# Delta-rule layer: SiLU of the values by Tanh, issued with the convolution instead of behind the exponentials

## Chip, cores and metric

The kernel runs on one core of a Trainium2 chip. The metric is the device time of one execution in microseconds (us). The engines are TensorE (PE, with its weight loads as PEld), VectorE (DVE), ScalarE (ACT), GpSimd (POOL) and the DMA queues (SyncE issues most of them, SPq).

## What is computed

One decoder layer in fp32: a gated delta-rule layer, a cross-attention over 77 context rows, and a mixture of eight experts, each followed by a layer norm. Only the first part matters here. For x of 4 sequences (B), 1024 tokens and 256 channels:

```python
def causal_conv_silu(x, w):
    B, T, C = x.shape
    K = w.shape[1]
    xp = jnp.pad(x, ((0, 0), (K - 1, 0), (0, 0)))
    y = sum((xp[:, i:i + T, :] * w[:, i] for i in range(K)))
    return jax.nn.silu(y)
...
q = causal_conv_silu(normed @ Wq, conv_q)
k = causal_conv_silu(normed @ Wk, conv_k)
v = causal_conv_silu(normed @ Wv, conv_v)
beta = jax.nn.sigmoid(normed @ Wb)
g = -jnp.exp(A_log) * jax.nn.softplus(normed @ Wa + dt_bias)
```

q and k are normalised, and then, token by token, with a state S per sequence and head (4 heads, keys of 64, values of 128):

```python
S = S * jnp.exp(g_t)[..., None, None]
v_eff = (v_t - jnp.einsum('bhk,bhkv->bhv', k_t, S)) * b_t[..., None]
S = S + k_t[..., None] * v_eff[..., None, :]
o_t = jnp.einsum('bhk,bhkv->bhv', q_t, S)
```

The output o is normalised, multiplied by the SiLU of a gate, and projected.

## The kernel before

The delta rule is worked out in eight slabs of 128 tokens, all four sequences at once. Within a slab the recurrence becomes matrix work: a triangular matrix of decays and key products is inverted, and its inverse is multiplied with keys, values and the state.

Each slab goes through generator functions, whose pieces `interleave` takes in turn (L244), so that the program's order mixes several of them. For slab i there are two phases (L840 to L851):

- the first phase: `prepares(i + 1)` (decay factors, an Exp on ScalarE at L495, and the products bp on VectorE, L518), `inverts(i)`, and a chain of `decays(i + 2)`, `values(i)` and `cumulated(i + 2)`. `decays` and `cumulated` hold further small Exps (L358, L369, L400).
- the second phase: `scans(i)` (the recurrence with the state), `blocks(i + 1)` (a long chain of small VectorE operations), `project(i + 2)` (queries and keys) and `normed(i + 3)`. Its ScalarE functions that are neither copies, scalings nor squares are Silus: of keys and queries (L435) and of the gate (L765).

`values` makes four tiles v[0] to v[3], one for each head, of 128 channels by 4 x 128 tokens. `convolve` (L275) makes a tile in two halves: matmuls into a PSUM bank (L281), the first of four taps on ScalarE (L291, an Identity with a per-channel scale), the other three on VectorE (L293, `scalar_tensor_tensor` of 128x256, in place). The weights of the taps are columns of the tile `cols`, read by channel. The Silu of the values is not part of `values`: it is issued by `silus` (L471) after the whole first phase, at L847.

Every Exp of L400 and L495 is kept in the list `exps`, and `silus` puts its four Silus behind them on ScalarE:

```python
with ExitStack() as behind:
    for e in exps:
        behind.enter_context(tc.issue_after(e.ins))
    exps.clear()
    for v in made["v"]:
        nc.scalar.activation(v, v, AF.Silu)
```

The order of instructions on each engine is otherwise settled by the framework's scheduler, from the order of the program and from when it expects operands and buffers[...].

What takes up the values is `scan` (L631). It first transposes queries and keys into a bank (L640, ptok) and the values into another (L643, pv; one transpose for each of v[0] to v[3]). Then VectorE makes qk from ptok and the factors qw (L646, qw itself copied from the cumulated exponentials at L409 and L410); ScalarE makes kd (L654, from ptok) and vt (L658, from pv), four each; TensorE turns qk (L664, pqd) and multiplies it with the inverse (L673, pwt); ScalarE copies both into padded tiles (L685); and then the products with the state follow (L691 on).

Squares of keys and queries, and the square and gate of the output, use a common buffer tag `sqr` with three buffers.

Of the kernel before, what the change touches and what calls it, by code (L numbers as in the profile page):

```python
# [10 lines left out]
F32 = mybir.dt.float32  # L11
I32 = mybir.dt.int32
AF = mybir.ActivationFunctionType
ALU = mybir.AluOpType
# [3 lines left out]
P = 128  # L18
B, T, D = 4, 1024, 256
NS = T // P  # L20
KC = D // P
H, HK, HV = 4, 64, 128
DV = H * HV
NCH = (2 * D + DV) // P
NQK = 2 * D // P
KCONV = 4
# [30 lines left out]
C_CONV = 2 * KC  # L57
# [53 lines left out]
def kernel(ctx: ExitStack, tc: tile.TileContext, a: dict, out: bass.AP):  # L111
    nc = tc.nc
    mm = nc.tensor.matmul

    def bc(ap, shape):
        return ap.to_broadcast(shape)
# [5 lines left out]
    def bank(name, tag="bank", bufs=None):  # L122
        kw = {} if bufs is None else {"bufs": bufs}
        return ps_pool[0].tile([P, 512], F32, tag=tag, name=name, **kw)
# [9 lines left out]
    wk = scan_scope.enter_context(tc.tile_pool(name="dwk", bufs=2))  # L134
# [25 lines left out]
    cols = const.tile([P, NCOLS], F32, name="cols")  # L160
# [83 lines left out]
    def interleave(*gens):  # L244

        gens = list(gens)
        while gens:
            for g in list(gens):
                if next(g, gens) is gens:
                    gens.remove(g)  # L250
# [9 lines left out]
    nc.vector.tensor_scalar(nega, nega, 1e30, -1.0, ALU.min, ALU.mult)  # L260


    state = []
    for b in range(B):
        s = wp.tile([P, 2, HV], F32, tag=f"state{b}", name=f"state{b}")
# [3 lines left out]
    for j in range(4):  # L269
        z = wp.tile([P, H, P], F32, tag=f"pad{j}", name=f"pad{j}")  # L270
        nc.vector.memset(z, 0.0)
        padded.append(z)
    before, exps = [], []

    def convolve(dst, c, nT):  # L275

        w0 = C_CONV + c * KCONV
        for j in range(2):
            pp = bank("pp")
            for kc in range(KC):  # L280
                mm(  # L281
                    pp[:, 0 : 2 * (HALO + P)],
                    lhsT=wqkv[:, kc, c * P : (c + 1) * P],
                    rhs=nT[:, kc, 2 * j : 2 * j + 2, :].rearrange("p b t -> p (b t)"),
                    start=kc == 0,
                    stop=kc == KC - 1,
                )
            yield
            pre = pp[:, 0 : 2 * (HALO + P)].rearrange("p (b t) -> p b t", b=2)
            ch = dst[:, 2 * j : 2 * j + 2, :]  # L290
            nc.scalar.activation(ch, pre[:, :, 0:P], AF.Identity, scale=cols[:, w0 : w0 + 1])  # L291
            for n in range(1, KCONV):
                nc.vector.scalar_tensor_tensor(  # L293
                    ch, pre[:, :, n : n + P], cols[:, w0 + n : w0 + n + 1], ch, ALU.mult, ALU.add
                )
# [89 lines left out]
    def cumulated(made):  # L385

        g = made["g"]
        pd = bank("pd")
        for n, m in enumerate((le, gt, ones)):
            mm(  # L390
                pd[:, n * B * H : (n + 1) * B * H],
                lhsT=m,
                rhs=g.rearrange("p b h -> p (b h)"),
                start=True,
                stop=True,
            )
        yield
        ex = slab.tile([P, 3, B, H], F32, tag="ex", name="ex")
        exps.append(
            nc.scalar.activation(ex.rearrange("p n b h -> p (n b h)"), pd[:, 0 : 3 * B * H], AF.Exp)  # L400
        )
        el = slab.tile([P, B, 2], F32, tag="el", name="el")
        whole = ex[:, 2].rearrange("p b (r q) -> p b r q", q=2)
        for par in range(2):
            h0 = par * HK
            nc.vector.tensor_copy(el[h0 : h0 + HK], whole[h0 : h0 + HK, :, :, par])

        qw = slab.tile([P, B, 2, H], F32, tag="qw", name="qw")
        nc.vector.tensor_copy(qw[:, :, 0, :], ex[:, 0])  # L409
        nc.vector.tensor_scalar_mul(qw[:, :, 1, :], ex[:, 0], -1.0)  # L410

        made.update(ex=ex, el=el, qw=qw)
# [52 lines left out]
        made.update(kq=kq, nb=nb, cd=cd, ik=ik, eq=eq)  # L465

    def values(made):
        made["v"] = v = [slab.tile([P, B, P], F32, tag=f"v{c}", name="v", bufs=1) for c in range(H)]
        for c in range(H):
            yield from convolve(v[c], NQK + c, made["nT"])  # L470
    def silus(made):  # L471

        with ExitStack() as behind:
            for e in exps:
                behind.enter_context(tc.issue_after(e.ins))
            exps.clear()
            for v in made["v"]:
                nc.scalar.activation(v, v, AF.Silu)

    def work(name, shape, **kw):  # L480
        return wk.tile(shape, F32, tag=name, name=name, **kw)

    def prepare(i, b, made):

        g, kq = made["g"], made["kq"]
        ee = work("ee", [P, H, 2, P])
        nc.gpsimd.tensor_tensor(
            ee[:, :, 1, :], bc(le.unsqueeze(1), [P, H, P]), bc(g[:, b, :].unsqueeze(2), [P, H, P]), ALU.mult
        )
        yield  # L490

        pe = bank("pe")
        mm(pe, lhsT=gt, rhs=ee[:, :, 1, :], start=True, stop=True)
        exps.append(
            nc.scalar.activation(ee[:, :, 0, :], pe.rearrange("p (h t) -> p h t", h=H), AF.Exp)  # L495
        )
        nc.gpsimd.tensor_tensor(
            ee[:, :, 1, :], ee[:, :, 0, :], bc(nge.unsqueeze(1), [P, H, P]), ALU.mult
        )
        yield  # L500

        bp = made["bp"]
        pks = [bank("pk") for par in range(2)]
        for r in range(2):
            for par, pk in enumerate(pks):
                h0 = slice(par * HK, (par + 1) * HK)
                mm(
                    pk[:, r * 2 * P : (r + 1) * 2 * P],
                    lhsT=kq[r][h0, 0, b, :],
                    rhs=kq[r][h0, :, b, :],  # L510
                    start=True,
                    stop=True,
                )
        yield
        for par, pk in enumerate(pks):
            for r in range(2):
                h = 2 * r + par
                nc.vector.scalar_tensor_tensor(  # L518
                    bp[:, :, b * H + h],
                    pk[:, r * 2 * P : (r + 1) * 2 * P].rearrange("p (n t) -> p n t", n=2),  # L520
                    made["nb"][:, b, h : h + 1],
                    ee[:, h],
                    ALU.mult,
                    ALU.mult,
                )
# [268 lines left out]
    made = [{} for _ in range(NS)]  # L794
# [6 lines left out]
    def prepares(i):  # L801
        made[i]["bp"] = slab.tile([P, 2, B * H, P], F32, tag="bp", name="bp", bufs=2)
        made[i]["tt"] = tts[i % 2]
        gens = [prepare(i, b, made[i]) for b in range(B)]
        return [chain(*gens[n::2]) for n in range(2)]

    def inverts(i):
        return [invert(b, made[i]) for b in range(0, B, 2)]

    def scans(i):  # L810
        return [
            chain(scan(i, b, made[i]), scan(i, b + 1, made[i])) for b in range(0, B, 2)
        ]
# [4 lines left out]
    def some(f, i, *args):  # L818
        return [f(*args, made[i])] if i < NS else []
# [15 lines left out]
    interleave(*some(decays, 0, 0), *some(normed, 1, 1))  # L835
    keys0 = project(0, made[0])
    interleave(chain(islice(keys0, 5), *some(cumulated, 0), keys0), *some(decays, 1, 1))
    interleave(*prepares(0), *some(cumulated, 1), *some(normed, 2, 2))
    interleave(blocks(0, made[0]), *some(project, 1, 1))
    for i in range(NS):  # L840
        ahead = prepares(i + 1) if i + 1 < NS else []
        interleave(
            *ahead,
            *inverts(i),
            chain(*some(decays, i + 2, i + 2), values(made[i]), *some(cumulated, i + 2)),
        )
        silus(made[i])  # L847
        if i + 1 < NS:
            interleave(
                *scans(i), *some(blocks, i + 1, i + 1), *some(project, i + 2, i + 2), *some(normed, i + 3, i + 3)  # L850
            )  # L851
# [820 lines left out]
```

## Time and profile before

| | |
|---|---|
| median of 3 runs | 1769.08 us (1767.61 to 1770.75) |
| the profiled execution | 1769.31 us, of which the span 1767.5 us |
| delta-rule stage | from the start to about 760 us |
| VectorE, taps of the values (L293) | 192, mean 478 ns, 81.7 us |
| ScalarE, Silu of the values (L478) | 32, median 629 ns |
| ScalarE, table loads in front of L478 / L495 / L435 | 7 / 8 / 4, each 1283 ns |
| last Exps and Silu table loads by slab | loads at 138.3, 231.5, 322.4, 412.8, 504.5, 592.6, 671.3 us |

The span is the time from the first to the last instruction in the trace; the execution's time has a little more around it. A row of the profile names the line of the code, the engine, the operation, and the tiles that it writes and reads. The releaser behind an idle time is what ended it. Several instructions of one line that run in a row are shown as one row with their number, so that 7.13 us for x18 is the time of all eighteen.

### The profile page before, as it was taken

The page shows a single profiled execution, that of the slowest core. Times are in us where ns is not written, and L with a number is a line of the kernel's source. Part 1 is how long each engine was busy: PE and PEld are TensorE (multiplying, and loading weights), DVE is VectorE, ACT ScalarE, POOL GpSimd, SP SyncE. Part 2 cuts the span into 40 slices and gives each one's busy share as a digit, 9 for nine tenths or more (in the row PEclk, how much of TensorE's full clock was granted, in tenths as well). Part 3 has the DMA queues.
Part 4 walks back from the last instruction along what each step waited for, and adds up shares of the span by engine and source line. Part 5 has one row for each costly group of instructions (what it writes and reads, how often), then busy time and mean ns, then how long its engine had stood idle before and what let it go on. Part 6 is the DMA issues. An engine that isn't in the chain of part 4 may idle for free. (4 is left out here: it accounts for less than half of the span.)

```text
span 1767.5 us, 28455 instructions
## 1 busy us (share of the span) xinstructions
PE 1593.5 (90%) x9524; PEld 1154.2 (65%) x9524; DVE 1176.1 (67%) x3557; ACT 938.1 (53%) x2216; POOL 565.4 (32%) x486
## 2 busy tenths in 40 slices
PE   6659999999999999896889999999989999999991
PEld 4247777676767667773667778778856666666660
DVE  4657686878787875735366888888865655554554
ACT  4425555555555554551288888788843333333333
POOL 2311212121212121015045666566733322222222
PEclk9868999999989998998999999999999999999995
DMA  4011101010101010203130011111353332222226
GB/s 142 19 19 22 40 19 43 19 43 19 43 19 31 19 31 19 56 7 125 44 147 13 27 44 43 40 43 37 126 189 70 64 47 47 46 46 46 47 32 199
DMA packets 119023, 94.20 MB, mean 53 GB/s; under 512 B 56939, under 2 KB 108639, under 8 KB 118367
## 3 DMA queue, kind: packets, MB, share of 16 engines
q1 hardware_dynamic: 102383, 71.39, 14.3%
q0 software_dynamic: 13296, 17.83, 6.0%
q10 hardware_dynamic: 3200, 3.15, 0.6%
q8 instruction: 78, 1.28, 0.3%
q14 instruction: 66, 0.54, 0.1%
HBM read 55.46 MB, written 36.90 MB: 52 GB/s over the span
## 5 line engine op out<-in xcount | busy, mean ns | idle before, releaser
L1547 POOL DMA_INDIRECT xd<-my,mrow x71 | 110.5, 1557 | 295.0 <-ACT my L1546 266.1
L1116 ACT ACTIVATE sc<-sc,ntop,rq 128x77 f32<-128x77 f32 x512 | 182.4, 447 | 5.2 <-DVE ntop L1111 4.6
L1147 PE MATMUL pxo<-ball,aT 128*128 128x256 f32 (+1 forms) x640 | 151.9, 385 | 1.5 <-DVE xs L1158 1.5
L281 PE MATMUL pp<-nT,wqkv 128*128 128x262 f32 x512 | 151.5, 434 | 0.2 <-PE pu L613 0.2
L1077 POOL TENSOR_TENSOR rq<-rq,nhalf 128x8 f32<-128x8 f32 x64 | 106.7, 1668 | 130.3 <-DVE rq L1076 129.2
L1498 PE MATMUL pgt<-wall,mxT 128*128 x284 | 135.4, 599 | 0.0
L1498 PE MATMUL pup<-wall,mxT 128*128 x284 | 134.4, 596 | 0.0
L1525 PE MATMUL pdn<-wdn,mhT 128*128 x568 | 134.2, 379 | 0.0
L752 POOL TENSOR_TENSOR so<-so,nhalf 128x4 f32<-128x4 f32 x32 | 32.5, 1017 | 309.5 <-DVE so L751 309.5
L1147 PEld LDWEIGHTS pxo<-ball,aT 128*128 128x128 f32 (+1 forms) x640 | 118.1, 193 | 15.8 <-DVE xs L1158 2.1
L1060 PE MATMUL pq<-wdn,xT 128*128 128x512 f32 x256 | 120.6, 594 | 1.5 <-ACT qsq L1070 1.0
L281 PEld LDWEIGHTS pp<-nT,wqkv 128*128 128x128 f32 x512 | 99.9, 211 | 23.4 <-issue 5.1
L293 DVE SCALAR_TENSOR_TENSOR kq<-pp,cols,kq 128x256 f32<-128x256 f32 x192 | 88.6, 479 | 36.3 <-ACT kq L291 33.9
L1525 PEld LDWEIGHTS pdn<-wdn,mhT 128*128 128x128 f32 x568 | 102.5, 190 | 11.0
L1506 DVE TENSOR_TENSOR sge<-pgt,ball 128x512 f32<-128x512 f32 x71 | 49.1, 692 | 86.4 <-PE pgt L1498 85.6
L1507 ACT ACTIVATE sge<-sge 128x512 f32<-128x512 f32 x71 | 44.7, 630 | 112.5 <-DVE sge L1506 112.4
L1498 PEld LDWEIGHTS pup<-wall,mxT 128*128 128x128 f32 x284 | 54.5, 192 | 69.0 <-issue 69.0
L1508 DVE TENSOR_TENSOR pup<-pup,ball 128x512 f32<-128x512 f32 x71 | 49.7, 700 | 69.8 <-PE pup L1498 69.3
L1125 POOL TENSOR_TENSOR sc<-sc,den 128x616 f32<-128x616 f32 x64 | 78.1, 1221 | 55.0 <-DVE den L1124 50.3
L1546 ACT ACTIVATE my<-my,mw 128x256 f32<-128x256 f32 x71 | 36.1, 508 | 106.3 <-DVE my L1545 106.3
L293 DVE SCALAR_TENSOR_TENSOR v<-pp,cols,v 128x256 f32<-128x256 f32 x192 | 81.7, 478 | 14.0 <-ACT v L291 13.3
L1096 PE MATMUL psc<-wdn,qT 128*128 128x154 f32 x512 | 78.7, 296 | 7.2 <-ACT qT L1088 7.2
(314 smaller groups left out, 3705.5 us busy)
## 6 DMA issues: line engine op xcount, KB each, us to landing
mx<-xg SPq DMA_DIRECT2D x71, 130.0 KB, 2.1
xs<-xd SPq DMA_DIRECT2D x12, 512.0 KB, 10.6
xi<-in_x SPq DMA_DIRECT2D x8, 512.0 KB, 4.5
am<-ab SPq DMA_DIRECT2D x16, 256.0 KB, 3.8
xd<-kd SPq DMA_DIRECT2D x32, 128.0 KB, 1.7
wall<-in_L_ffn_gate_w SPq DMA_DIRECT2D x8, 512.0 KB, 9.6
wall<-in_L_ffn_up_w SPq DMA_DIRECT2D x8, 512.0 KB, 10.2
xd<-xs SPq DMA_DIRECT2D x8, 512.0 KB, 4.1
```

Source lines behind the costliest of these rows:

```text
L281: mm(pp[:, 0 : 2 * (HALO + P)], lhsT=wqkv[:, kc, c * P : (c + 1) * P], rhs=nT[:, kc, 2 * j : 2 * j + 2, :].rearrange("p b t -> p (b t)"), ...
L293: nc.vector.scalar_tensor_tensor(ch, pre[:, :, n : n + P], cols[:, w0 + n : w0 + n + 1], ch, ALU.mult, ALU.add)
L1060: mm(pq, lhsT=t["xT"][:, kc, :], rhs=xwq[:, kc, c0 : c0 + HH * XD], start=kc == 0, stop=kc == KC - 1,)
L1077: nc.gpsimd.tensor_tensor(rq, rq, nhalf[:, :HH], ALU.pow)
L1096: mm(ps[:, c * 2 * SC : (c + 1) * 2 * SC], lhsT=qT[:, 2 * g + c, :], rhs=kbd[:, b, half * XC // 2 + 2 * g + c, :], start=True, stop=True,)
L1116: nc.scalar.activation(sc[:, h], sc[:, h], AF.Exp, scale=t["rq"][:, h : h + 1], bias=t["ntop"][:, h : h + 1])
L1125: nc.gpsimd.tensor_tensor(sc, sc, bc(den.unsqueeze(2), [P, HH, SC]), ALU.mult)
L1147: mm(px[:, 0:D], lhsT=aT[:w, c, :], rhs=vo[:w, b, half * NV + c, :], start=half == 0 and c == 0, stop=half == 1 and c == NV - 1,)
L1498: mm(ps, lhsT=t["xT"][:, c, :], rhs=wall[:, bass.ds(e * EW + off + c * FF, FF)], start=c == 0, stop=c == KC - 1,)
L1508: nc.vector.tensor_tensor(pu, pu, ball[:, bass.ds(e * FF + B_U, FF)], ALU.add)
L1525: mm(px[:, 0:D], lhsT=t["hT"][:, f, :], rhs=wdn[:, bass.ds(e * EV + f * D, D)], start=f == 0, stop=f == FC - 1,)
L1547: nc.gpsimd.indirect_dma_start(out=xd, out_offset=bass.IndirectOffsetOnAxis(ap=row, axis=0), in_=y, in_offset=None, compute_op=ALU.add,)
```

## The change

The taps of the values are halved once at the start, so that `convolve` yields y, half of the convolution. The SiLU of 2y is y + y tanh(y). Right after each tile's convolution, inside `values`, a Tanh on ScalarE writes a new tile th (tag `sqr`), and a `scalar_tensor_tensor` on VectorE writes (th + 1) * v into v. The list of the exponentials and `silus` go.

```diff
--- before.py
+++ after.py
@@ -260,6 +260,10 @@
     nc.vector.tensor_scalar(nega, nega, 1e30, -1.0, ALU.min, ALU.mult)
 
 
+    vw = cols[:, C_CONV + NQK * KCONV : C_CONV + (NQK + H) * KCONV]
+    nc.vector.tensor_scalar_mul(vw, vw, 0.5)
+
+
     state = []
     for b in range(B):
         s = wp.tile([P, 2, HV], F32, tag=f"state{b}", name=f"state{b}")
@@ -270,7 +274,7 @@
         z = wp.tile([P, H, P], F32, tag=f"pad{j}", name=f"pad{j}")
         nc.vector.memset(z, 0.0)
         padded.append(z)
-    before, exps = [], []
+    before = []
 
     def convolve(dst, c, nT):
 
@@ -396,9 +400,7 @@
             )
         yield
         ex = slab.tile([P, 3, B, H], F32, tag="ex", name="ex")
-        exps.append(
-            nc.scalar.activation(ex.rearrange("p n b h -> p (n b h)"), pd[:, 0 : 3 * B * H], AF.Exp)
-        )
+        nc.scalar.activation(ex.rearrange("p n b h -> p (n b h)"), pd[:, 0 : 3 * B * H], AF.Exp)
         el = slab.tile([P, B, 2], F32, tag="el", name="el")
         whole = ex[:, 2].rearrange("p b (r q) -> p b r q", q=2)
         for par in range(2):
@@ -465,17 +467,13 @@
         made.update(kq=kq, nb=nb, cd=cd, ik=ik, eq=eq)
 
     def values(made):
+
         made["v"] = v = [slab.tile([P, B, P], F32, tag=f"v{c}", name="v", bufs=1) for c in range(H)]
         for c in range(H):
             yield from convolve(v[c], NQK + c, made["nT"])
-    def silus(made):
-
-        with ExitStack() as behind:
-            for e in exps:
-                behind.enter_context(tc.issue_after(e.ins))
-            exps.clear()
-            for v in made["v"]:
-                nc.scalar.activation(v, v, AF.Silu)
+            th = wk.tile([P, B, P], F32, tag="sqr", name="th", bufs=3)
+            nc.scalar.activation(th, v[c], AF.Tanh)
+            nc.vector.scalar_tensor_tensor(v[c], th, 1.0, v[c], ALU.add, ALU.mult)
 
     def work(name, shape, **kw):
         return wk.tile(shape, F32, tag=name, name=name, **kw)
@@ -491,9 +489,7 @@
 
         pe = bank("pe")
         mm(pe, lhsT=gt, rhs=ee[:, :, 1, :], start=True, stop=True)
-        exps.append(
-            nc.scalar.activation(ee[:, :, 0, :], pe.rearrange("p (h t) -> p h t", h=H), AF.Exp)
-        )
+        nc.scalar.activation(ee[:, :, 0, :], pe.rearrange("p (h t) -> p h t", h=H), AF.Exp)
         nc.gpsimd.tensor_tensor(
             ee[:, :, 1, :], ee[:, :, 0, :], bc(nge.unsqueeze(1), [P, H, P]), ALU.mult
         )
@@ -844,7 +840,6 @@
             *inverts(i),
             chain(*some(decays, i + 2, i + 2), values(made[i]), *some(cumulated, i + 2)),
         )
-        silus(made[i])
         if i + 1 < NS:
             interleave(
                 *scans(i), *some(blocks, i + 1, i + 1), *some(project, i + 2, i + 2), *some(normed, i + 3, i + 3)
```

## Prediction

> **What bounds the kernel now.** I read the page first, then the waits of the delta-rule stage (0 to 760 us, the only stage that the change touches), then the windows around one slab boundary, then the timeline of that boundary. The chain that ended last is of no use here: it only covers the last few instructions of the kernel.
>
> The page says that TensorE carries the span:
>
> ```profile
> span 1767.5 us, 28455 instructions
> PE 1593.5 (90%) x9524; PEld 1154.2 (65%) x9524; DVE 1176.1 (67%) x3557; ACT 938.1 (53%) x2216; POOL 565.4 (32%) x486
> ```
>
> So time is only to be had, or lost, where PE stands still. The waits of the stage name two such places behind the Silus of the values (L478), and the qk product that PE needs next has a row of its own:
>
> ```profile
> PEld pv L643 <- ACT v L478: 24.4, 18, 2.0
> PE pv L643 <- ACT v L478: 18.7, 14, 1.8
> PEld pqd L664 <- DVE qk L646: 12.5, 12, 1.7
> PE pqd L664 <- DVE qk L646: 5.8, 9, 0.8
> ```
>
> The columns are total us, times, longest. The loads and the matmuls of one wait are the same idle stretch, so the Silu wait is worth 19 to 24 us of PE in the whole stage, about 3 us for each of eight slabs. The windows of 5 us around the second boundary (columns: length, then PE, PEld, DVE, ACT, POOL busy, granted clock, DMA share, GB/s) say which engine is late there:
>
> ```profile
> 220.00:225.00 5.00, 5.00 (x53) 4.08 (x52) 4.76 (x14) 2.32 (x5) 2.49 (x2) 1.00 0.00 0
> 225.00:230.00 5.00, 5.00 (x24) 4.22 (x23) 5.00 (x15) 2.11 (x5) 1.47 (x2) 1.00 0.00 0
> 230.00:235.00 5.00, 3.39 (x24) 2.71 (x23) 5.00 (x14) 4.00 (x7) 0.61 (x1) 1.00 0.50 71
> 235.00:240.00 5.00, 2.88 (x20) 1.49 (x20) 4.85 (x15) 3.53 (x13) 0.00 (x0) 0.92 0.33 90
> 240.00:245.00 5.00, 5.00 (x34) 4.34 (x34) 2.20 (x10) 4.83 (x16) 0.00 (x0) 0.74 0.01 2
> ```
>
> PE loses 1.6 + 2.1 us in the third and fourth row, and in these rows VectorE is full (5.00 and 4.85 of 5), as it has been for 10 us before. ScalarE has room. The timeline of that boundary shows the order (columns: start, us, then idle before and its releaser):
>
> ```profile
> 229.35 7.13 DVE L293 SCALAR_TENSOR_TENSOR v<-pp,cols,v 128x256 f32<-128x256 f32 x18
> ...
> 231.24 0.21 ACT L400 ACTIVATE ex<-pd 128x48 f32<-128x48 f32 x1
> 231.47 1.28 ACT L478 ACT_TABLE_LOAD   x1
> ...
> 232.76 1.15 ACT L478 ACTIVATE v<-v 128x512 f32<-128x512 f32 x2
> ...
> 236.52 0.63 ACT L478 ACTIVATE v<-v 128x512 f32<-128x512 f32 x1 [0.28 <-DVE v L293]
> ...
> 236.90 1.28 DVE L646 TENSOR_TENSOR qk<-ptok,qw 128x512 f32<-128x512 f32 x2
> ...
> 237.20 0.44 PE L643 MATMUL pv<-sq,v 128*128 128x128 f32 x2 [1.47 <-ACT v L478]
> ...
> 237.57 0.37 ACT L658 ACTIVATE vt<-pv,ik 128x128 f32<-128x128 f32 x1 [0.42 <-PE pv L643]
> ```
>
> The table load at 231.47 and the first two Silus are done by 233.9. The last Silu does not wait for the exponentials: it starts 0.04 us after the last convolution step of v[3] on VectorE (229.35 + 7.13 = 236.48). And qk starts as soon as VectorE is through with the same queue and a few small copies. So at this boundary the wait that ends last is VectorE's chain of convolution steps, not the wait behind the exponentials.
>
> **The change, part by part.**
>
> *Scaling of the weights.* One VectorE instruction on 128x16 at the start: 0.17 us by rows of that shape, 100 us ahead of the first use at 123.8, in a start-up in which VectorE waits 7.2 us for the weights wo alone (L831). Nothing; 0.2 us without that cover.
>
> *ScalarE at the boundary.* 32 Silus of 0.63 us become 32 Tanhs. No row shows a Tanh; the nearest is the Silu itself, same shape and engine, and I take its 0.63. Bounds: 0.60 (Silu L765, 128x512) and 0.63, so nothing either way. The seven table loads of L478 (1.283 us each, 9.0 in all) leave the boundary. They do not vanish: the first Silu behind it (L435, at 247.0 here) needs the load instead. Between 245 and 250 us ScalarE is busy 2.67 of 5 us, so I take 0 for it; the other end is all of it, 7 x 1.28 = 9.0.
>
> *Are there more loads?* This is the rule that speaks against putting another function among the Exps: the Trainium skill, "ScalarE: Activation LUTs", section "Table sets: the hidden batching unit", wants activations batched by table set, not spread out. But the same section puts tanh into the set of exp, so Tanh beside Exp needs no load. Its section "What ACT_TABLE_LOAD costs" prices a switch at 2.66 us with a drain; here the load is 1.28 us and the Silu follows it at once (231.47 + 1.28 = 232.75, Silu at 232.76), so the trace's 1.28 decides: the 7 moved loads are at stake with 9.0, not 18.6 us. If Tanh did not share the set, 28 Tanhs could cost two loads each, 28 x 2 x 1.28 = 72 us; no run shows a Tanh, so this rests on the page, and I take 0. In the last slab there is no Exp, and Tanh then falls between Silus: 0, or two loads, 2.6 us; I take 0, as Square, Copy and Identity too run beside both without a load.
>
> *VectorE.* New are 32 products (th + 1) * v on 128x512, four in each slab. The nearest row is the qk product L646 of that shape: 0.68 us alone, 1.28 for two in a row, so 0.64 in a full queue; it reads PSUM, the new one SBUF. The skill's "VectorE: DVE Perf Modes" (section "Mode 2×_2P — use both read ports for one tensor") says that a two-tensor fp32 operation can't use the double rate, so half of this would be wrong; its table of cycles gives (512 + 8 + 150)/0.96 = 0.70 us, four for 2.8 us instead of 2.56. I take the row. 32 x 0.64 = 20.5 us more VectorE work.
>
> Where does it lie? v[0] has its last convolution step only at 226.6, and from 223 to 238 VectorE has no gap: there is no cover for it. The products of v[0] to v[2], 3 x 0.64 = 1.9 us, come before qk in the program's order, and qk moves back by that. The product of v[3] waits for its Tanh (0.63), during which the small copies and the first qk run. So at the boundary of the trace: last convolution step 236.48 + 1.9 = 238.4; Tanh to 239.1; first qk until 237.55 + 1.9 = 239.5; product of v[3] until 240.2; pv at 240.25 instead of 237.20. ScalarE's run of vt, kd and padding copies (237.57 to 244.28, without a gap) can begin with kd, which only needs qk: at 239.5, 1.9 us later; for vt it is about 3. I take 2.5 for a boundary of this kind.
>
> *The eight boundaries.* Three are like the one shown (231, 413 and 505 us: last Silu at once behind VectorE): 3 x 2.5 = 7.5. At 593 the last Silu ran 0.7 us behind VectorE, since a kq step (L291) that waited for PE stood ahead of it in ScalarE's queue: 1.6. At 138 and 323 that kq step held the Silu up by 2.4 to 2.5 us (VectorE done at 142.2, Silu at 144.48); here the early Tanh takes that wait away, and VectorE gives back a little more: Tanh to 144.8, product behind the first qk to 145.9, pv at 145.9 instead of 145.15, and kd can fill in: 0.5 each, 1.0. At 671 and 740 VectorE has gaps (3.50 busy of 10 us from 680): the products of v[0] and v[1] vanish in them, and what is left is one product and one more handover for v[3]: 1.0 each, 2.0. Sum: 7.5 + 1.6 + 1.0 + 2.0 = 12.1 us.
>
> *Waits that are added.* Each product waits on VectorE for its Tanh; queued behind it are the next tile's convolution steps, the el and qw copies, qk, and then the bp and ut work. Each Tanh waits on ScalarE for VectorE; behind it stand the L291 steps, which free PE's banks. In the trace L291 runs 4 us ahead of VectorE, so that one costs nothing. If the products stand directly behind their own tile, VectorE stalls 0.63 + 2 x 0.05 = 0.7 us at each; I take 0 for v[0] to v[2], since other tiles' steps are ready to stand between, and keep 32 x 0.7 = 23 us as the far end. The th tile takes one of three buffers that the squares and gates share: these are idle at this time, 0. PE, GpSimd and the DMA queues get no new instruction; the store of bp to the scratch (L540, 229.46) is behind bp L518, which precedes the products.
>
> *What PE does with it.* Outside the boundaries PE is full (5.00 of 5 in nearly every window from 240 to 265), so what a boundary loses is not made up later. The profiled execution took 1769.31 (span 1767.5 and 1.8 around it); 1769.3 + 12.1 = 1781.4. The median of the runs is 1769.1, 0.2 below; I say 1781.
>
> **The rivals.**
>
> *A. VectorE's queue gets longer (my forecast), 1781.* For it: VectorE has no gap where PE has them. Own range 1774 to 1790: one product in four hidden, or the moved loads in full (9.0) on top.
>
> *B. ScalarE was the bound, faster.* The mechanism: with the load and the Silus off the end, pv of v[0] to v[2] go at once, and qk is ordered ahead of the last convolution steps, as it is at 681 us in the trace; it is decided by where qk stands in VectorE's queue. For it: 19 to 24 us of PE's waits are named after L478. Against it: v[3] was bound by VectorE at five boundaries. If each of seven boundaries gets 1.3 us back, the load, it is 9 us: 1760; if all of the wait, 1745.
>
> *C. No difference.* The products cost 12, the removed waits give as much: 138 and 323 would each have to gain 2.4 us and the others stay level: 1769.
>
> *D. Handover stalls.* Every product waits in place for its Tanh: 1781 + 23 = 1804.
>
> **How the numbers follow.** A 0.58, B 0.22, C 0.13, D 0.07. A measurement of this kernel can tell about 0.2%, 3.5 us, from no change. Faster is B, 0.23 with a little of C; same is C with the low edge of A, 0.14; slower is the rest of A and D, 0.63. The range goes from 1757 (most of B) to 1794 (A with both its terms high); outside are the far end of B and D.
>
> **What would show it.** In the profile after: products of 128x512 at 0.64 to 0.68 us, 32 of them; table loads as many as before, the L478 ones now at L435 or L765; the waits of pv on ACT gone and in their place waits of pv on the new product; VectorE full from 220 to 241 us and PE's idle there about 2 us more. I am wrong if qk starts as early after the exponentials (L400) as before, that is 5.7 us, if loads multiply, or if PE's waits at 138 and 323 shrink by over 2 us.

## The result, and the profile after

The changed kernel takes 1783.23 us (median of 5 runs, 1781.98 to 1786.31) against 1768.61 us for the kernel before: ratio 1.0078, 95% interval 1.0062 to 1.0093. It is slower, by 14.6 us. The profiled execution has a span of 1781.4 us against 1767.5 us, 13.9 us more. From the page of the changed kernel:

```profile
span 1781.4 us, 28502 instructions
PE 1605.5 (90%) x9524; PEld 1154.2 (65%) x9524; DVE 1197.2 (67%) x3590; ACT 938.3 (53%) x2216; POOL 565.5 (32%) x486
```

TensorE's work is the same (9524 matmuls), and yet its busy time is 12.0 us longer; where that comes from is counted further down. VectorE has 33 instructions and 21.1 us more (1176.1 to 1197.2). ScalarE is level.

The waits of the delta-rule stage (columns as before):

```profile
ACT th L475 <- DVE v L297: 50.4, 28, 3.2
...
PEld pqd L660 <- DVE qk L642: 13.3, 8, 2.1
...
PE pqd L660 <- DVE qk L642: 11.9, 8, 1.9
...
PEld pv L639 <- DVE v L476: 9.4, 12, 2.6
...
PE pv L639 <- DVE v L476: 5.7, 12, 2.4
```

The wait of pv on ScalarE (19 to 24 us before) is gone. In its place stands a smaller one on the new product (L476), and the wait of pqd on qk has doubled on PE, from 5.8 to 11.9 us (on PEld it went from 12.5 to 13.3). These waits are now on VectorE. The first row is the Tanh that waits for VectorE, too. But the waits named here have become shorter in sum, not longer, so the loss can't be read from them alone.

The same boundary as in the prediction, in windows of 5 us (it comes 1.4 us earlier here, since the slab began 1.4 us earlier):

```profile
220.00:225.00 5.00, 5.00 (x30) 3.77 (x30) 4.86 (x17) 1.56 (x4) 0.00 (x0) 1.00 0.00 0
225.00:230.00 5.00, 4.05 (x24) 3.34 (x22) 5.00 (x14) 2.47 (x6) 2.08 (x2) 1.00 0.31 46
230.00:235.00 5.00, 3.08 (x14) 1.64 (x13) 5.00 (x12) 1.45 (x4) 0.00 (x0) 1.00 0.46 116
235.00:240.00 5.00, 3.32 (x14) 1.87 (x14) 4.78 (x16) 2.94 (x11) 0.00 (x0) 0.61 0.00 0
240.00:245.00 5.00, 5.00 (x32) 4.14 (x31) 3.22 (x14) 4.63 (x16) 0.00 (x0) 0.71 0.00 0
```

VectorE is full or nearly so in the first four rows; PE stands still for 0.95 + 1.92 + 1.68 = 4.6 us. In the five rows of before it was 1.61 + 2.12 = 3.7 us, so this is 0.8 us more, not the 2 us that the prediction named. The clock column lost more: (0.39 + 0.29) x 5 = 3.4 us here, (0.08 + 0.26) x 5 = 1.7 us before. And the timeline of that boundary:

```profile
230.15 0.19 ACT L403 ACTIVATE ex<-pd 128x48 f32<-128x48 f32 x1
...
233.62 0.69 DVE L476 SCALAR_TENSOR_TENSOR v<-th,v 128x512 f32<-128x512 f32 x1
...
235.38 0.48 DVE L297 SCALAR_TENSOR_TENSOR v<-pp,cols,v 128x256 f32<-128x256 f32 x1
...
235.94 0.69 DVE L642 TENSOR_TENSOR qk<-ptok,qw 128x512 f32<-128x512 f32 x1
235.96 0.63 ACT L475 ACTIVATE th<-v 128x512 f32<-128x512 f32 x1 [1.32 <-DVE v L297]
236.62 0.69 DVE L476 SCALAR_TENSOR_TENSOR v<-th,v 128x512 f32<-128x512 f32 x1
...
236.68 0.69 PE L660 MATMUL pqd<-sq,qk 128*128 128x128 f32 x2 [1.87 <-DVE qk L642]
...
238.34 0.69 PE L639 MATMUL pv<-sq,v 128*128 128x128 f32 x2
238.86 1.14 ACT L654 ACTIVATE vt<-pv,ik 128x128 f32<-128x128 f32 x4 [1.03 <-PE pv L639]
...
247.40 1.28 ACT L437 ACT_TABLE_LOAD   x1
```

The order is the one forecast: products of v[0] to v[2] ahead of qk, that of v[3] behind the first qk and its Tanh (235.94, 235.96, 236.62). The table load stands at the first Silu behind the boundary.

### The profile page after: what moved, and what is told of

Read it like the earlier page. It is cut to its first block, busy times and chain, and to the rows that moved or that the text cites. A ratio compares the mean times of both kernels' runs of the same rounds, so it can differ in the third digit from the quotient of the medians.

```text
span 1781.4 us, 28502 instructions
## 1 busy us (share of the span) xinstructions
PE 1605.5 (90%) x9524; PEld 1154.2 (65%) x9524; DVE 1197.2 (67%) x3590; ACT 938.3 (53%) x2216; POOL 565.5 (32%) x486
## 5 line engine op out<-in xcount | busy, mean ns | idle before, releaser
L1501 DVE TENSOR_TENSOR sge<-pgt,ball 128x512 f32<-128x512 f32 x71 | 49.1, 692 | 86.4 <-PE pgt L1493 85.6
L1502 ACT ACTIVATE sge<-sge 128x512 f32<-128x512 f32 x71 | 44.7, 630 | 112.8 <-DVE sge L1501 112.7
## 6 DMA issues: line engine op xcount, KB each, us to landing
wall<-in_L_ffn_gate_w SPq DMA_DIRECT2D x8, 512.0 KB, 10.2
```

## Experiments

Three theories were set against each other. Theory 1: the products make VectorE's queue longer, and qk and pv stand behind it (the forecast). Theory 2: ScalarE's order, since the early Tanh waits with the next tiles' first taps queued behind it. Theory 3: the granted clock of TensorE, which falls in the gaps. Ratios are to the kernel before on the same chip, with 95% intervals.

**The place without the product.** Edit to the changed kernel:

```diff
-            th = wk.tile([P, B, P], F32, tag="sqr", name="th", bufs=3)
-            nc.scalar.activation(th, v[c], AF.Tanh)
-            nc.vector.scalar_tensor_tensor(v[c], th, 1.0, v[c], ALU.add, ALU.mult)
+            nc.scalar.activation(v[c], v[c], AF.Tanh)
```

> Tanh as early as in the changed kernel, in place, and no product: v becomes tanh of half of the convolution, so the values are wrong by the left-out y + y tanh(y). Theory 1 (VectorE's queue: the product stands ahead of qk at the boundary and costs the time): with the product gone the loss goes too, and the table load and the Silus are off the boundary as well: 1760 to 1769. Theory 2 (ScalarE's order: the early Tanh waits 3.2 us for VectorE with the first-tap steps of the next tiles queued behind it): the loss stays, 1779 to 1784. Theory 3 (the granted clock of TensorE: more of it is lost at the boundary, whatever the engine): between them, and the clock loss summed over the eight slabs says where.

Measured: 1769.21 us, ratio 0.9985 (0.9970 to 1.0000). The loss is gone: theory 2 falls. But there is hardly a gain either: with Tanh, taking the wait behind the exponentials away is worth 0 to 0.3%, and the time lies at the upper edge of what theory 1 had.

**The product without the place.** Edit to the kernel before:

```diff
             yield from convolve(v[c], NQK + c, made["nT"])
+            th = wk.tile([P, B, P], F32, tag="sqr", name="th", bufs=3)
+            nc.vector.scalar_tensor_tensor(th, v[c], 1.0, v[c], ALU.add, ALU.mult)
```

> The kernel before, with a product of the same size after each tile's convolution, written to a scratch tile and not used; Silus stay behind the exponentials. Theory 1: the added VectorE time alone gives the loss, 1779 to 1785. Theory 2: no change, 1767 to 1771.

Measured: 1782.73 us, ratio 1.0071 (1.0050 to 1.0091). An unused product of the same size, in the old order, makes the whole loss. With the run before, this settles that the added product on VectorE is the cause of the loss and the early place is not.

**Tanh and product at the old place.** Edit to the kernel before (with the halved taps):

```diff
             for v in made["v"]:
-                nc.scalar.activation(v, v, AF.Silu)
+                th = wk.tile([P, B, P], F32, tag="sqr", name="th", bufs=3)
+                nc.scalar.activation(th, v, AF.Tanh)
+                nc.vector.scalar_tensor_tensor(v, th, 1.0, v, ALU.add, ALU.mult)
```

> Arithmetic of the changed kernel (Tanh and product), at the old place, behind all exponentials. Theory 1: at least as slow as the changed kernel, 1781 to 1788, as each product still stands ahead of pv, and later. Theory 2: the order of before, so most of the loss goes, 1769 to 1774.

Measured: 1779.72 us, ratio 1.0050 (1.0032 to 1.0068). Most of the loss is there without the early place, as theory 1 has it. I had expected it to be at least as slow as the changed kernel, 1781 to 1788; it is if anything a little faster, and the intervals overlap.

**The product on GpSimd.** Edit to the changed kernel:

```diff
-            nc.vector.scalar_tensor_tensor(v[c], th, 1.0, v[c], ALU.add, ALU.mult)
+            nc.gpsimd.tensor_tensor(th, th, v[c], ALU.mult)
+            nc.gpsimd.tensor_tensor(v[c], v[c], th, ALU.add)
```

> The changed kernel with the product as two GpSimd operations (th times v, then added to v), about 2.2 to 2.6 us for each tile against VectorE's 0.65. Theory 1: VectorE gets its time back, qk starts early, only pv of the last tile comes some 1.7 us later: 1764 to 1774. Theory 2: no better than the changed kernel, 1780 to 1786.

Measured: 1802.99 us, ratio 1.0181 (1.0160 to 1.0202), a miss of the expectation. VectorE's busy time falls only from 1197.2 to 1189.8 us, with 1176.1 in the kernel before. The two operations take 1.27 us each, so that v[3] comes later still, and VectorE's own instructions run longer beside them. From the timeline of this kernel's boundary:

```profile
235.46 1.34 DVE L408 COPY el<-ex 64x8 f32<-64x8 f32 x2
235.51 1.26 POOL L477 TENSOR_TENSOR v<-v,th 128x512 f32<-128x512 f32 x1
...
236.98 1.28 DVE L643 TENSOR_TENSOR qk<-ptok,qw 128x512 f32<-128x512 f32 x2
```

The two copies of 64x8 took 0.33 us at this place before; here they end with the GpSimd operation (236.80 and 236.77), and qk waits behind them. So the run doesn't test theory 1 cleanly.

**qk ahead of the last value tile.** In both kernels the key and query transposes, qk and kd move out of `scan` into a function `opened`, which `values` calls for the first and third sequence:

```diff
+            if c == 3:
+                for b in (0, 2):
+                    opened(b, made)
             yield from convolve(v[c], NQK + c, made["nT"])
```

> The kernel before, with the key and query transposes, qk and kd of the first and third sequence issued ahead of the last value tile's convolution instead of behind it. Nothing is left out. Theory 1 (what counts at the boundary is where VectorE's queue has qk): ScalarE's kd and padding copies, some 5 us of its run of 6.7, move ahead of the last tile and into time in which it idles, while v[3] comes 1.3 us later: 1 to 2.5 us for each of eight boundaries, 1752 to 1765. Theory 3 (the granted clock): as far as PE's gaps get shorter the clock loss falls too, then the low end of it. If VectorE's queue doesn't matter: 1770.

> The changed kernel with the same reordering. Theory 1: the same gain from its own level of 1783, so 1764 to 1777, and still 10 to 14 us behind the same reordering of the kernel before, since the products' time remains. Theory 2: no gain.

Measured: the kernel before goes to 1750.94 us, ratio 0.9898 (0.9878 to 0.9918); the changed one to 1776.54 us, ratio 1.0037 (1.0022 to 1.0052), 7 us under its 1783. Each gain was expected, but not their difference: with this order the changed kernel is 25.6 us behind, where 10 to 14 were expected. So the products cost more here than in the order of before. From the timeline of the reordered kernel before, at its second boundary:

```profile
224.63 1.28 DVE L643 TENSOR_TENSOR qk<-ptok,qw 128x512 f32<-128x512 f32 x2
...
225.91 1.73 ACT L651 ACTIVATE kd<-ptok,cd 128x64 f32<-128x64 f32 x8
...
229.69 0.44 PE L667 MATMUL pv<-sq,v 128*128 128x128 f32 x2
...
230.19 2.18 ACT L671 ACTIVATE vt<-pv,ik 128x128 f32<-128x128 f32 x8
...
231.20 1.05 PE L704 MATMUL py<-vt,tt 128*128 128x128 f32 x8
```

kd is done while the last tile is still being convolved, and py starts 1.5 us after the last pv instead of some 5.5 us (237.20 and 242.75 before). So when qk is issued counts, as theory 1 says; but the edit moves qk together with kd and the transposes ahead of them, and doesn't say which of them gains the time.

**Silu early.** The kernel before with each Silu in `values`, right behind its convolution, and `silus` gone:

```diff
             yield from convolve(v[c], NQK + c, made["nT"])
+            nc.scalar.activation(v[c], v[c], AF.Silu)
...
-        silus(made[i])
```

> The kernel before, with each Silu right after its tile's convolution and not behind the exponentials. Nothing is left out. It shows what Tanh buys over Silu at that place: Silu and Exp do not share a table, so loads of 1.283 us multiply. Theory 1: VectorE's queue is as before, the loads (up to four more for each of seven slabs) fall into ScalarE's slack in part: 1772 to 1790.

Measured: 1753.51 us, ratio 0.9905 (0.9887 to 0.9923): faster than the kernel before, far off the expectation. It has 36 table loads in the stage against 22, and ScalarE is busy 954.1 us against 938.1; what the 14 more loads cost doesn't show in the total. Its activation stands at the place of the early Tanh alone, and yet it is 0.8% faster by the ratios (some 14 us). Besides function and loads, one thing differs: behind most boundaries the scheduler put a few VectorE instructions (`state` and `so`) in another order. The windows at the second boundary, first of early Tanh alone, then of early Silu, each beginning some 5 us ahead of the last value tile:

```profile
228.00:233.00 5.00, 4.06 (x25) 2.73 (x23) 5.00 (x14) 1.96 (x5) 0.01 (x1) 1.00 0.60 110
233.00:238.00 5.00, 2.75 (x20) 1.77 (x22) 4.76 (x17) 3.91 (x16) 0.00 (x0) 0.81 0.13 42
238.00:243.00 5.00, 5.00 (x23) 4.27 (x20) 2.23 (x10) 4.00 (x13) 0.00 (x0) 0.50 0.00 0
```

```profile
225.00:230.00 5.00, 4.10 (x27) 3.23 (x25) 5.00 (x14) 4.26 (x7) 0.00 (x0) 1.00 0.54 105
230.00:235.00 5.00, 3.28 (x27) 1.98 (x27) 4.77 (x17) 4.58 (x17) 0.00 (x0) 1.00 0.16 45
235.00:240.00 5.00, 5.00 (x44) 4.82 (x43) 2.28 (x10) 4.83 (x14) 0.00 (x0) 1.00 0.00 0
```

VectorE is as full in both. PE stands still for 2.25 us in the middle row of the first and 1.72 us in that of the second, and only in the first the granted clock falls, to 0.50 over the whole third row. This is where theory 3 comes in. That the clock makes the difference between the two is argued from this, not shown.

**PE kept busy in the gaps.** 24 matmul calls for each slab, whose results are overwritten, among the value transposes of the first sequence. The trace shows two PE instructions for each (9908 in all, against 9524):

```diff
         for c in range(H):
+            for _ in range(8 if b == 0 and c else 0):
+                mm(pv[:, c * P : (c + 1) * P], lhsT=ident, rhs=made["v"][c - 1][:, b, :], start=True, stop=True)
```

> The changed kernel with 24 matmuls of 128x128 for each slab that compute nothing needed, written to the pv bank ahead of the transposes of the first sequence, to fill PE's gaps at the boundary. Theory 3: with the gaps filled, the granted clock stays at 1.00 behind the boundary and up to 3.4 us for each slab come back: 1758 to 1775. Theory 1 without the clock: 24 x 8 matmuls more on the engine that bounds, no gain, 1783 to 1795.

> The kernel before with the same 24 filling matmuls for each slab. If the clock made the difference between the two kernels (theory 3 in full), both come to the same time when kept warm: 1768 to 1772, as the changed kernel did (1771). If the products' time on VectorE makes it (theory 1) and the clock comes on top for both, the kernel before gains 6 to 12 us as well: 1757 to 1763, some 10 us ahead of the changed kernel kept warm.

> Early Tanh without the product (the values are wrong by the left-out product), with the filling matmuls. Theory 1: the changed kernel kept warm minus the products' time: 1756 to 1763, level with the kernel before kept warm. If the place of the Tanh itself costs something that the clock hid: 1764 to 1771.

Measured: the changed kernel 1771.38 us, ratio 1.0010 (0.9995 to 1.0025), so 192 useless calls make it about 12 us faster. The kernel before 1770.37 us, ratio 1.0007 (0.9990 to 1.0023), no gain; early Tanh alone 1764.45 us, ratio 0.9966 (0.9954 to 0.9979), just above what theory 1 had. The first two are level, as theory 3 in full would have it. But the comparison isn't clean: in the kernel before the first three tiles come close together behind the table load, so the fillers find less of a gap in front of them. From the starts of the slabs to their first py, in one profile of each (the sums of the table below), the time is 10 us longer with fillers in the kernel before (316.3 to 326.4) and 12 us shorter in the changed one (335.6 to 323.5). So a filler can cost as much as it gives, and the two kernels being level doesn't decide between the theories.

**Both orders together.** Silu early and qk first, without and with fillers:

> The kernel before with both orders that helped: each Silu right behind its tile's convolution, with its own table loads, and qk and kd ahead of the last value tile. Nothing is left out. If the two gains (16 and 18 us) are the same gap shortened twice, no better than one alone, 1746 to 1754; if they add, 1735 to 1745.

> The same with the filling matmuls. Theory 3: what clock loss is left (about 36 us summed over the slabs in each of the two) falls by another 8 to 12: 5 to 10 us faster than without them. Theory 1 without the clock: no faster, or slower by up to 10 for the added matmuls.

Measured: 1751.62 us, ratio 0.9903 (0.9886 to 0.9919), and 1759.84 us, ratio 0.9952 (0.9936 to 0.9967). The two gains do not add, as if both shortened the same gap. With the fillers it is 8 us slower, where theory 3 had 5 to 10 us faster. The fastest kernels of the study are qk first, early Silu and both together, level with each other and about 1% faster than the kernel before.

## Why the prediction was right, and where not

**Size and cause.** 1781 was forecast, 1783 measured, and the cause is the forecast one: the products' time on VectorE. The work was sized at 20.5 us and is 21.1; the product at 0.64 to 0.68 us and is 0.69 (median, in the row of its line), so the estimate of 0.70 that the prediction set aside was nearer for a single one:

```profile
L476 DVE SCALAR_TENSOR_TENSOR v<-th,v x32: 681/690/1164, 133.2 to 762.9; 128x512 f32<-128x512 f32 x32
```

The product alone gives 1.0071, the place alone 0.9985, both 1.0078. So the cause is shown. How the loss comes together from the single boundaries is another matter: there the sum came out right partly by luck.

**The boundary shown.** The forecast moved the pv of v[3] by 3.05 us and the first qk by 1.9. Measured from the start of the slab (the first transposes of the inverse, at 200.0 before and 198.6 after), that pv comes 2.6 us later, py 1.7 us, and qk only 0.5 us (236.90 before, 235.94 here). This was the first sign that the prediction had named for being wrong: qk starts 5.8 us after the last small Exp (230.15), hardly more than the 5.7 of before. The last taps end 0.8 us later and not 1.9. Over all eight boundaries qk does come later, by 0.5 to 4.3 us from the start of its slab, so the mechanism stands, but the term of 1.9 was not what happened at the boundary from which it was taken. The term of 2.5 for the loss there held on the average of the three boundaries of this kind (table below).

**The eight boundaries.** The time from that start to the first py, by slab, before and after, and what was forecast:

| slab's boundary (before) | before | after | more | forecast |
|---|---|---|---|---|
| 138 | 44.1 | 44.1 | 0.0 | 0.5 |
| 231 | 42.8 | 44.5 | 1.7 | 2.5 |
| 323 | 44.5 | 45.0 | 0.5 | 0.5 |
| 413 | 41.7 | 44.7 | 3.0 | 2.5 |
| 505 | 42.6 | 44.9 | 2.3 | 2.5 |
| 593 | 38.4 | 44.9 | 6.5 | 1.6 |
| 671 | 36.3 | 38.6 | 2.3 | 1.0 |
| 740 | 25.9 | 29.0 | 3.1 | 1.0 |
| sum | 316.3 | 335.6 | 19.3 | 12.1 |

Five terms are within 0.8 us. Three are wrong. At 593 the forecast is 5 us short. Windows of that boundary, kernel before:

```profile
595.00:600.00 5.00, 3.04 (x26) 2.12 (x23) 4.87 (x15) 3.33 (x12) 0.00 (x0) 1.00 0.26 72
600.00:605.00 5.00, 5.00 (x42) 4.45 (x43) 1.99 (x9) 4.83 (x18) 0.00 (x0) 1.00 0.01 3
605.00:610.00 5.00, 5.00 (x48) 4.59 (x47) 4.38 (x16) 3.12 (x6) 0.00 (x0) 1.00 0.00 0
```

and the changed one:

```profile
600.00:605.00 5.00, 2.35 (x9) 1.22 (x9) 4.95 (x15) 1.54 (x3) 0.00 (x0) 0.97 0.44 105
605.00:610.00 5.00, 4.72 (x23) 2.74 (x23) 4.65 (x15) 3.90 (x17) 0.00 (x0) 0.50 0.01 3
610.00:615.00 5.00, 5.00 (x35) 4.67 (x36) 3.38 (x14) 3.81 (x11) 0.00 (x0) 0.85 0.01 2
```

Before, this boundary was the only one of the first six that passed without a fall of the clock. With the products PE stands still for 2.65 us in one row, and the next row has half the clock. But the clock behind the boundary isn't where most of the 6.5 us come from. The same slab, cut at the end of the last taps, from its start and up to py, kernel before and changed one:

```profile
563.49:596.54 33.05, 30.87 (x361) 24.36 (x359) 26.44 (x78) 17.14 (x32) 10.11 (x10) 0.95 0.14 33
596.54:601.93 5.39, 3.43 (x29) 2.23 (x27) 4.98 (x19) 4.69 (x19) 0.00 (x0) 1.00 0.02 5
```

```profile
566.75:604.47 37.72, 33.57 (x361) 25.89 (x359) 29.29 (x84) 16.15 (x32) 10.10 (x10) 0.91 0.13 29
604.47:611.64 7.17, 6.36 (x26) 4.06 (x27) 6.62 (x23) 5.93 (x22) 0.00 (x0) 0.52 0.01 3
```

The last taps end 4.7 us later, before the clock falls at the boundary; only 1.8 us are added behind them. In the kernel before, this slab's taps ended 33.1 us after its start, those of the five slabs ahead of it 35.3 to 36.5, so it lost a lead that the others never had. The lower clock ahead of the taps' end is a part of it (0.05 x 33.05 = 1.7 us before, 0.09 x 37.72 = 3.4 after); the rest stays open. At 671 and 740 the forecast let the products of v[0] and v[1] vanish in VectorE's gaps: 2.0 us in sum against 5.4. There the last taps end 0.8 and 1.9 us later, so they don't all vanish, and behind the taps 1.5 and 1.3 us are added for v[3], where 1.0 was taken.

**What was forecast as lost is partly given back.** From py to the next slab the changed kernel is faster, by 5.4 us in all (382.5 to 377.1). I had said that a boundary's loss isn't made up. In two slabs (138 and 413, 1.8 and 1.6 us) it is so since before the half clock lasted beyond py there; the rest, 0.4 to 0.6 in each of five slabs, I can't name. So that the sum of 12.1 came near the 13.9 of the spans is partly luck, since two errors stood against each other: 7.2 us too little ahead of py, and 5.4 us given back behind it that were taken as nothing.

**The clock as a term.** The prediction names the clock column but gives it no price. With (1 - granted clock) times length, summed from about 107 us to the end of the stage, one profile of each gives 44.0 us before and 50.8 after, and PE's idle time 51.4 and 53.0. A lower clock counts only while PE is busy: this part is 42.5 us before and 45.9 after. So of the 13.8 us more in the stage, 1.6 are idle time and 3.4 the clock. The other 8.7 us are longer busy time at full clock for the same matmuls, nearly all of it in rows that stand at the boundaries (pwt, pp, pv, py, ptok). A matmul that stands alone has a longer record than one in a row: two pv took 0.44 us and eight py 1.05 in the rows shown, so what is issued piece by piece counts as busy. The unused product in the old order loses as much in another mixture (7.2 idle, 5.4 clock, 0.9 the rest). The two kernels with qk first differ by only 3.1 us in the clock and yet by 25.6 us in time. So by these counts a lower clock is 3 to 5 us of the loss and not the whole of it, whatever the fillers seem to say. The sum is 49.1 for early Tanh alone and 37.0 for early Silu.

**ScalarE.** The loads did move and not multiply: before 7 at L478 and 4 at L435, after 10 at L437 and 1 at L761, and 27 in the whole kernel in both. Tanh needs none of its own, among the Exps, as the Trainium skill ("ScalarE: Activation LUTs", section "Table sets: the hidden batching unit") has it, nor among the Silus of the last slab, where the prediction had left 2.6 us open. That the moved load costs nothing holds: at the boundary shown it delays the first square of the output (L744) by 1.3 us, but the gate product comes 13.1 us after py as before. The same section's rule to batch by table set was no guide to the time here: the early Silu has 14 loads more and is 0.9% faster than the kernel before.

**The early Tanh in ScalarE's queue.** At the longest it waited 3.2 us for VectorE, with three first taps behind it, which I had priced at nothing. Early Tanh alone, which has these waits too, is no slower than the kernel before; but it also has the early place, so what the wait costs by itself isn't shown.

**The rivals.** B: the gain of freeing pv of v[0] to v[2] is 0 to 0.3% with early Tanh alone and 0.8 to 1.1% with early Silu, so B held more than the forecast gave it; the products outweighed it. And the point that B named, qk ahead of the last taps, is a real one: with kd it is worth 1.0% when it is done, and the change didn't do it. D: no product waited in place for its Tanh (0.3 us once in the stage).

## What to carry to other kernels

Here an edit that took a wait off the end of one engine's queue, at the price of work on an engine whose queue is full at that very place, was slower, although the engine that paid looked idle on average: VectorE's share was 67%, and 21 us more of its time (1.2% of the span) cost 0.8% of the kernel's. Look in windows of a few microseconds for what is full while the bound engine stands still, and ask first whether the order in that queue can be changed; here moving qk and kd of two sequences ahead gave as much as any other edit, 1.0%. Price a table load by the room of its engine at that place: a kernel with 14 more of them was among the fastest. And when a sum over boundaries comes out right, measure it boundary by boundary: here two errors of 7.2 and 5.4 us hid behind it.

## What the runs showed of the hardware

- PE's clock fell behind stretches of 5 us in which PE stood still for 1.9 to 2.7 us in several gaps, and stayed at 1.00 behind others with 1.7 to 2.0 us, so no sharp limit shows in these windows; it then stood at 0.50 for some 3.4, 6.8 or 10.2 us. A gap's price is therefore not its length: fillers in the gaps made the changed kernel 12 us faster, and one with short gaps 8 us slower. The Trainium skill ("TensorE: Matmul & The Clock Gate", section "HAM oscillation — how this bites in real kernels") puts the limit at gaps over about 3.4 us; between 108 and 800 us, where the clock fell in every slab, the longest single gap is 2.1 us before and 2.7 us after.
- A VectorE copy of 64x8 took up to 1.18 us instead of 0.17 while a GpSimd operation on SBUF ran, and ended with it, in six of its sixteen runs. In the changed kernel one of the 32 products took 1.16 instead of 0.69 us; a GpSimd operation on `ee` ran during its first 0.6 us.
- ScalarE kept its order even where a later instruction was ready. In the kernel before, at 138 us, the taps of v[3] end at 142.2, but a kq step ahead of the last Silu waits for PE until 144.1:

```profile
144.10 0.47 ACT L291 ACTIVATE kq<-pp,cols 128x256 f32<-128x256 f32 x1 [2.88 <-PE pp L281]
144.48 0.62 ACT L478 ACTIVATE v<-v 128x512 f32<-128x512 f32 x1
```
